# Loading two weights later and folding them inside the adjacency loop, in a graph layer followed by attention and experts

## The chip, the cores and the metric

The kernel runs on one core of one Trainium2 chip. The metric is the device time of one execution in microseconds (us), reported as the median of several runs. The core has five engines that run side by side, each through its own list of instructions in order: TensorE (PE in the profile; PEld is its weight load), VectorE (DVE), ScalarE (ACT), GpSimd (POOL) and SyncE (SP, which here only issues transfers). They wait for each other and for transfers on semaphores.

## The reference, cut to what matters

One layer takes x of 4096 nodes by 256 features and an adjacency matrix of 4096 by 4096. It has a graph part and then an attention part with a mixture of eight experts:

```
f   = layernorm(x)                                  # 4096 x 256
h   = adj @ (f @ neigh_W.T) / (adj.sum(axis=1) + 1)
x   = x + concat([f, h]) @ lin_W.T                  # = f @ L1 + h @ L2
x   = x + attention_and_experts(layernorm(x))
```

With lin_W.T split into its upper half L1 and its lower half L2, the second term is (adj @ f / deg) @ (neigh_W.T @ L2). The product of the two 256 x 256 weights does not depend on the data, so the kernel computes M = neigh_W.T @ L2 once. This product is what the change calls folding.

## The kernel before, in words

The graph part is written in manual order: each engine executes its instructions in the order in which the Python code emits them. The nodes are cut into NB = 8 blocks of 512 (four tiles of 128). An outer loop `aggregate(b, steps)` (L474) goes over the eight blocks of result nodes, and inside it the index jb goes over the eight blocks of neighbours. For each pair one block of adjacencies, 512 x 512 in float32 (1 MB), is loaded into one of three buffers (`load`, L258), and TensorE multiplies it with the normalised features of block jb. The product is arranged as seven products of 256 x 256 pieces in place of eight, which needs sums and differences of the pieces:

- `halve(n)` (L430) makes the sums and differences of adjacency block n on DVE (L441 to L444, 128 x 512 each). POOL adds the same sums up for the degrees (L449, L451).
- `halve_x(b)` (L403) does the same for the features of block b (L406 to L409).

Before a feature block can be used it has to be prepared. All of this happens during the first outer pass, b = 0:

- `load_x(b)` (L255) loads 512 rows of x.
- `scales_x(b)` (L385) takes the statistics: `stats` on DVE (L162, L164), then `power` on POOL (L168, L169), which gives 1/standard deviation.
- `normed_x(b, t)` (L391, instruction L393) normalises tile t on DVE.
- `turned_x(b)` (L398) transposes the normalised block on TensorE (L379), and ACT copies the result out of PSUM (L381).
- `features(b)` (L458) multiplies the transposed block with L1 on TensorE (L465, tiles pf, two halves). Between these matmuls it emits the four `normed_x` of block b + 1, and after each half DVE adds the result to x (L472).

In pass b = 0 the steps of preparation sit in the middle of each neighbour block, after the fourth of its seven products. At jb they are: `halve(jb + 1)`, `turned_x(jb + 2)`, `features(jb + 2)`, `halve_x(jb + 2)`, `scales_x(jb + 4)`. The step of jb = 3 also has `load_rest`, which issues seven small loads for the attention part. In the fourth block the features at hand are therefore those of block 5, and the neighbours whose `normed_x` stand in between are those of block 6.

`fold()` (L341) makes M in two halves: four matmul instructions L345 in the source (tiles pm; the trace shows eight passes, since a float32 matmul is recorded as two), and two copies L349 on ACT into m_sb. M is first used when the result of b = 0 is finished, during b = 1. The tiles pm and pf share one PSUM pool of two buffers, `p_pj`, with the tag "pj": a new tile takes the older of the two buffers, and its first matmul must wait until the last reader of the tile that was there is done. For a pf tile that reader is the DVE addition L472.

Before the loop the order is: first loads, then 26 transposes of the identity (L620, tile idle) which compute nothing that is used, then `fold()`, then blocks 0 and 1 of the features with the statistics of blocks 1, 2 and 3 and the sums of adjacency block 0. The weight neigh_W lies in qT[4] and L2 in qT[5], which are not used otherwise before the fifth result block is worked on or, for qT[5], before `turn_wo` in the step of jb = 6.

Transfers are issued by two engines: SP (x, adjacencies, neigh_W) and ACT (L2, L1). The instruction that issues may have to wait for a semaphore, and then everything behind it on that engine waits.

Of the kernel before, what the change touches and what calls it, by code (L numbers as in the profile page):

```python
# [17 lines left out]
P = 128  # L18
N = 4096
C = 256  # L20
# [46 lines left out]
def fast_kernel(  # L67
# [24 lines left out]
    nc = tc.nc  # L92
# [65 lines left out]
    def stats(pool, b, tiles=range(TB)):  # L158

        st = pool.tile([P, TB, nc.vector.BN_STATS_DIM], F32, tag="st", name=f"st_{b}_{tiles[0]}")  # L160
        for t in tiles:
            nc.vector.bn_stats(st[:, t, :], res[b][:, t, :])  # L162
        for t in tiles:
            nc.vector.bn_aggr(mv[b][:, t, :], st[:, t, :])  # L164

    def power(dst, src, scale, eps):

        nc.gpsimd.tensor_scalar(dst, src, scale, eps, op0=ALU.mult, op1=ALU.add)  # L168
        nc.gpsimd.tensor_tensor(dst, dst, half[:, 0 : dst.shape[1]], op=ALU.pow)  # L169
# [73 lines left out]
    with (  # L243
# [11 lines left out]
        def load_x(b):  # L255
            nc.sync.dma_start(res[b], x_blocks[b])

        def load(n):  # L258

            if n < NB * NB:  # L260
                blocks[n] = adjs.tile([P, TB, 512], F32, tag="a", name=f"a_{n // NB}_{n % NB}")
                nc.sync.dma_start(blocks[n], adj[n // NB, n % NB])
# [3 lines left out]
            nc.sync.dma_start(res[0][:, some], x_blocks[0][:, some])  # L266

        wn_sb, l2_sb = qT[4][:, :, 0:C], qT[5][:, :, 0:C]
        nc.sync.dma_start(wn_sb, neigh_w.rearrange("(c p) o -> p c o", p=P))
        nc.scalar.dma_start(l2_sb, lin_t[C : 2 * C, :].rearrange("(c p) o -> p c o", p=P))  # L270

        m_sb = gw.tile([P, 2, C], F32, name="m_sb")
        l1_sb = qT[6][:, :, 0:C]
# [1 line left out]
        for n in range(2):  # L275
            load_x(1 + n)
            load(n)
        for b in range(3, 6):
            load_x(b)
        tables = {}  # L280

# [59 lines left out]
        def fold():  # L341
            for c in range(2):
                pm = p_pj.tile([P, 512], F32, tag="pj", name=f"pm_{c}")
                for k in range(2):
                    nc.tensor.matmul(  # L345
                        pm[:, :C], wn_sb[:, k, c * P : (c + 1) * P], l2_sb[:, k, :],
                        start=(k == 0), stop=(k == 1),
                    )
                nc.scalar.copy(m_sb[:, c, :], pm[:, :C])  # L349
# [23 lines left out]
        def transposed(src, dst):  # L373

            for h in range(2):
                tr = p_tr.tile([P, 2, 2, P], F32, tag="tr", name="tr")
                for t in range(2):
                    for c in range(2):
                        nc.tensor.transpose(tr[:, c, t, :], src(2 * h + t, c), ident)  # L379
                cols = slice(h * 2 * P, (h + 1) * 2 * P)  # L380
                nc.scalar.copy(dst[:, :, cols], tr.rearrange("p c t i -> p c (t i)"))  # L381
# [3 lines left out]
        def scales_x(b, at_a_time=TB):  # L385
            for t in range(0, TB, at_a_time):
                some = slice(t, t + at_a_time)
                stats(gx, b, range(TB)[some])
                power(rstd[b][:, some], mv[b][:, some, 1:2], 1.0, EPS_LN)
# [8 lines left out]
        def turned_x(b):  # L398

            turned[b] = qT[b % 4]  # L400
            transposed(lambda t, c: g[b][:, t // 2 * 2 + c, t % 2, :], turned[b])

        def halve_x(b):  # L403

            part = [g[b][:, k] for k in range(7)]
            nc.vector.tensor_sub(part[T1], part[G12], part[G11])  # L406
            nc.vector.tensor_sub(part[T3], part[G22], part[G12])
            nc.vector.tensor_sub(part[T2], part[G22], part[T1])
            nc.vector.tensor_sub(part[T4], part[T2], part[G21])  # L409
# [20 lines left out]
        def halve(n):  # L430

            if n == NB * NB:
                return
            a = blocks.pop(n)
            m = {
                f"A{r + 1}{k + 1}": a[:, 2 * k : 2 * k + 2, r * 2 * P : (r + 1) * 2 * P]
                for r in range(2) for k in range(2)
            }
            m["S1"], m["S2"], m["S4"] = sums_at[n % 2]
            m["S3"] = m["A21"]  # L440
            nc.vector.tensor_add(m["S1"], m["A21"], m["A22"])  # L441
            nc.vector.tensor_sub(m["S2"], m["S1"], m["A11"])
            nc.vector.tensor_sub(m["S4"], m["A12"], m["S2"])  # L443
            nc.vector.tensor_sub(m["S3"], m["A11"], m["A21"])  # L444
            halves_of[n] = m
            jb = n % NB
            for i, k in ((0, 2), (1, 0)):
                if jb == 1:
                    nc.gpsimd.tensor_add(all_s[:, i], sums_at[(n - 1) % 2][k], sums_at[n % 2][k])  # L449
                elif jb > 1:  # L450
                    nc.gpsimd.tensor_add(all_s[:, i], all_s[:, i], sums_at[n % 2][k])  # L451
            if jb == NB - 1:

                ends = all_s[:, :, 0, :]
                nc.gpsimd.tensor_add(ends, ends, all_s[:, :, 1, :])
                nc.gpsimd.tensor_add(ends[:, 0], ends[:, 0], ends[:, 1])

        def features(b):  # L458
            fT = turned.pop(b)
            for h in range(2):  # L460
                pj = p_pj.tile([P, 2, C], F32, tag="pj", name=f"pf_{b}_{h}")
                for t in range(2):
                    for c in range(2):
                        at = (2 * h + t) * P
                        nc.tensor.matmul(  # L465
                            pj[:, t, :], fT[:, c, at : at + P], l1_sb[:, c, :],
                            start=(c == 0), stop=(c == 1),
                        )
                    if b + 1 < NB:
                        normed_x(b + 1, 2 * h + t)  # L470
                x1 = res[b][:, 2 * h : 2 * h + 2, :]
                nc.vector.tensor_add(x1, x1, pj)  # L472
# [145 lines left out]
        idle = p_pj.tile([P, TB, P], F32, tag="pj", name="idle")  # L618
        for n in range(26):
            nc.tensor.transpose(idle[:, n % TB], ident, ident)  # L620
        fold()
        load(2)
        for b in range(6, NB):
            load_x(b)
# [2 lines left out]
        features(0)  # L627
        halve_x(0)
        turned_x(1)
        scales_x(2)  # L630
        halve(0)
        features(1)
        halve_x(1)
        scales_x(3)
        steps = {jb: [] for jb in range(NB)}
        for jb in range(NB):
            for f, b in (
# [2 lines left out]
            ):  # L640
                if b < NB or f is halve:
                    steps[jb].append(lambda f=f, b=b: f(b))
        steps[3].append(load_rest)
        for jb, f in ((5, scale_rest), (6, turn_wo), (7, router_wo)):
            steps[jb].append(f)
        behind, at_end = [], []
        for b in range(NB):
            sums, degrees, linear = finish(b)
            if b:

                steps = {0: behind, (0, "end"): at_end}
# [1489 lines left out]
@with_exitstack  # L2141
def adj_ffn_kernel(ctx: ExitStack, tc: tile.TileContext, *args):
    nc = tc.nc
    kept = ctx.enter_context(tc.tile_pool(name="kept", bufs=1))
    left_over = kept.tile([1, 1], I32, name="left_over")
    table = kept.tile([P, 2, RARE], I32, name="rare_table")
    mine = kept.tile([P, RARE, NE], F32, name="rare_mine")
    lists = fast_kernel(tc, *args, left_over, table, mine)
    state = nc.values_load(left_over[0:1, 0:1], min_val=0, max_val=2)
    with tc.If(state != 0):  # L2150
        with tc.If(state == 2):
            general_kernel(tc, *args)
        with tc.If(state == 1):
            ln2, w13, w2, out = (args[i] for i in (8, 9, 10, 13))
            rare_groups(tc, ln2, w13, w2, out, lists, table, mine)
# [73 lines left out]
```

## Time and profile before

| | before |
|---|---|
| time, median of 3 runs | 1600.92 us (1599.28 to 1603.71) |
| profiled execution | 1608.9 us, span 1607.1 us |
| TensorE busy | 1584.9 us, 99% of the span |
| DVE busy | 1069.7 us, 67% |
| POOL busy | 617.4 us, 38% |
| ACT busy | 473.3 us, 29% |
| mean DMA rate over the span | 130 GB/s |

Busy time is the time in which an engine executes something, not the time in which it is at its peak. The shares are means over the whole span. For TensorE in the stretch from 30 to 60 us, where the features are prepared, the profile gives 29.17 us busy, and for DVE 29.38 us; from 200 to 300 us it is 100.00 and 70.60.

A row of the timeline gives the start and the length of a group of equal instructions that follow each other on an engine, the engine, the source line, the operation and its operands, how many there were, and, in brackets, how long the engine was idle before the group and what released it. "pf<-qT_all" means that tile pf is written from tile qT_all.

### The profile page before, as it was taken

The page shows a single profiled execution, that of the slowest core. Times are in us where ns is not written, and L with a number is a line of the kernel's source. Part 1 is how long each engine was busy: PE and PEld are TensorE (multiplying, and loading weights), DVE is VectorE, ACT ScalarE, POOL GpSimd, SP SyncE. Part 2 cuts the span into 40 slices and gives each one's busy share as a digit, 9 for nine tenths or more (in the row PEclk, how much of TensorE's full clock was granted, in tenths as well). Part 3 has the DMA queues.
Part 4 walks back from the last instruction along what each step waited for, and adds up shares of the span by engine and source line. Part 5 has one row for each costly group of instructions (what it writes and reads, how often), then busy time and mean ns, then how long its engine had stood idle before and what let it go on. Part 6 is the DMA issues. An engine that isn't in the chain of part 4 may idle for free. (4 is left out here: it accounts for less than half of the span.)

```text
span 1607.1 us, 22624 instructions
## 1 busy us (share of the span) xinstructions
PE 1584.9 (99%) x8404; PEld 1139.2 (71%) x8404; DVE 1069.7 (67%) x2055; ACT 473.3 (29%) x893; POOL 617.4 (38%) x726
## 2 busy tenths in 40 slices
PE   9999999999999999999999999999999999999997
PEld 8888888888888543344343434348889999989996
DVE  8966676676676688789889788884445453434443
ACT  1101001010010455554555545543112222222221
POOL 3445556556557341253433352412512222112113
PEclk9999999999999999999999999999999999999999
DMA  6333433434333000010100010176665776777784
GB/s 229 125 135 137 156 131 135 140 129 157 135 134 109 4 1 1 13 41 28 36 20 27 14 41 28 38 225 220 218 200 169 232 254 221 239 254 220 244 272 104
DMA packets 67991, 209.58 MB, mean 130 GB/s; under 512 B 14688, under 2 KB 46816, under 8 KB 54240
## 3 DMA queue, kind: packets, MB, share of 16 engines
q1 hardware_dynamic: 54608, 190.05, 34.1%
q0 software_dynamic: 12720, 17.47, 5.5%
q8 instruction: 68, 1.11, 0.3%
q10 hardware_dynamic: 544, 0.52, 0.1%
q14 instruction: 51, 0.42, 0.1%
HBM read 180.81 MB, written 31.42 MB: 132 GB/s over the span
## 5 line engine op out<-in xcount | busy, mean ns | idle before, releaser
L711 DVE TENSOR_TENSOR sum<-sum,pt 128x1024 f32<-128x1024 f32 (+3 forms) x258 | 298.1, 1155 | 17.7 <-ACT pt L693 0.5
L693 ACT ACTIVATE pt<-sc 128x1024 f32<-128x1024 f32 (+3 forms) x288 | 252.4, 958 | 177.5 <-PE sc L688 117.1
L688 PE MATMUL sc<-qT_all,kT 64*128 64x512 f32 (+3 forms) x1152 | 250.4, 569 | 1.4 <-ACT pt L693 0.4
L496 PE MATMUL acc<-a,g 128*128 128x256 f32 x1024 | 245.1, 380 | 0.0
L723 PE MATMUL ya<-pt,vv 128*64 128x512 f32 (+3 forms) x1152 | 242.6, 563 | 0.0
L1301 PE MATMUL h<-xT,qT_all 128*128 128x256 f32 (+1 forms) x1232 | 221.3, 339 | 0.7 <-DMA qT_all<-in_w_dram 0.7
L496 PEld LDWEIGHTS acc<-a,g 128*128 128x128 f32 x1024 | 193.4, 190 | 31.8 <-DVE vv L514 1.2
L1373 POOL DMA_INDIRECT acc_dram<-y,rows x57 | 89.8, 1575 | 317.1 <-DVE y L1368 85.1
L1301 PEld LDWEIGHTS h<-xT,qT_all 128*128 128x128 f32 x1232 | 196.5, 191 | 21.2 <-issue 2.3
L688 PEld LDWEIGHTS sc<-qT_all,kT 64*128 64x128 f32 x1152 | 103.8, 186 | 141.2 <-issue 107.5
L1308 DVE TENSOR_TENSOR hT<-si,h 128x256 f32<-128x256 f32 (+2 forms) x126 | 62.6, 507 | 185.8 <-ACT si L1307 184.2
L723 PEld LDWEIGHTS ya<-pt,vv 128*64 128x64 f32 x1152 | 76.2, 136 | 146.9 <-issue 139.8
L451 POOL TENSOR_TENSOR all_s<-all_s,more_sums 128x512 f32<-128x512 f32 x72 | 106.1, 1486 | 107.3 <-DVE more_sums L443 107.3
L1307 ACT ACTIVATE si<-h 128x256 f32<-128x256 f32 (+2 forms) x126 | 56.9, 453 | 281.6 <-PE h L1301 255.6
L496 PE MATMUL acc<-more_sums,g 128*128 128x256 f32 x512 | 126.2, 379 | 0.0
L907 POOL DMA_INDIRECT lists<-row,slots x64 | 70.7, 1105 | 115.8 <-issue 115.4
L1301 PE MATMUL h<-xT,res_all 128*128 128x256 f32 (+1 forms) x616 | 108.2, 334 | 0.0
L496 PEld LDWEIGHTS acc<-more_sums,g 128*128 128x128 f32 x512 | 97.2, 190 | 14.8
L1301 PEld LDWEIGHTS h<-xT,res_all 128*128 128x128 f32 x616 | 96.6, 191 | 9.0
L695 POOL TENSOR_SCALAR_AFFINE_SELECT pt<-pt 128x256 f32<-128x256 f32 x64 | 46.6, 754 | 116.0 <-ACT pt L693 115.2
L381 ACT COPY qT_all<-tr 128x512 f32<-128x512 f32 x30 | 16.1, 589 | 214.3 <-PE tr L379 214.3
L496 PE MATMUL acc<-qT_all,g 128*128 128x256 f32 x256 | 65.7, 379 | 0.0
(279 smaller groups left out, 2123.5 us busy)
## 6 DMA issues: line engine op xcount, KB each, us to landing
a<-in_adj_dram SPq DMA_DIRECT2D x64, 1024.0 KB
qT_all<-in_w_dram SPq DMA_DIRECT2D x28, 1408.0 KB
res_all<-in_w_dram SPq DMA_DIRECT2D x28, 768.0 KB
res_all<-in_w_dram SPq DMA_DIRECT2D x14, 1408.0 KB
qT_all<-in_w_dram SPq DMA_DIRECT2D x14, 768.0 KB
rows<-lists SPq DMA_DIRECT2D x25, 265.0 KB
lists<-pad SPq DMA_DIRECT2D x8, 662.5 KB
acc_dram<-res_all SPq DMA_DIRECT2D x8, 512.0 KB
```

The source lines that it names most:

```text
L451: nc.gpsimd.tensor_add(all_s[:, i], all_s[:, i], sums_at[n % 2][k])
L496: nc.tensor.matmul(acc[bank][:, at, :], g[jb][:, right, k, :], m[left][:, k, :], start=(jb == 0 and k == 0 and at == 0), stop=(jb == NB - ...
L688: nc.tensor.matmul(ps[:, j, :w], kT[sb][hd, i * P : (i + 1) * P], qT[b][hd, p, off:], start=True, stop=True,)
L693: nc.scalar.activation(pt[:, :, :w], ps[:, :, :w], AF.Exp, scale=HD ** -0.5)
L695: nc.gpsimd.affine_select(out=pt[:, :, 0:P], in_=pt[:, :, 0:P], pattern=[[0, 2], [1, P]], compare_op=ALU.is_ge, fill=0.0, base=0, channel_ ...
L711: nc.vector.tensor_add(sums[b, p][:, :, off:], before[:, :, off:], pt[:, :, : 512 - off])
L723: nc.tensor.matmul(accs[b, p][hd, off:], vv[sb][:, i, hd], pt[:, j, : 512 - off], start=(s == 0), stop=(s == TB * b + TB - 1),)
L907: put = nc.gpsimd.indirect_dma_start(out=lists[:, :], out_offset=bass.IndirectOffsetOnAxis(ap=chosen[b][:, k, t, :], axis=0), in_=flats[b] ...
L1301: nc.tensor.matmul(ps[:, m % 2, m // 2 - q, :], w13_sb[:, c, m * P : (m + 1) * P], xT[:, c, :], start=(c == 0), stop=(c == 1),)
L1307: nc.scalar.activation(si[:, 0:both, :], ps[:, 0, 0:both, :], AF.Silu)
L1308: nc.vector.tensor_mul(hT[:, q : q + both, :], si[:, 0:both, :], ps[:, 1, 0:both, :])
L1373: put = nc.gpsimd.indirect_dma_start(out=(acc_dram if k < NM - LAST else out)[:, :], out_offset=at, in_=y[:, h, :], in_offset=None, comput ...
```

## The change

It has four edits. The load of neigh_W moves from SP to ACT, and the loads of neigh_W and L2 are emitted after the loads of x blocks 1 to 3 and adjacency blocks 0 and 1; on ACT, the load of L1 now stands first. The call of `fold()` moves from the place ahead of block 0's transposes to the end of the step of jb = 3 (the fourth block of neighbours) in the first outer pass. `halve(0)` moves ahead of `scales_x(2)`, so DVE makes the first sums of adjacencies before the statistics of x block 2. The remaining line is only the x load of block 3, written apart.

```diff
-        nc.sync.dma_start(wn_sb, neigh_w.rearrange("(c p) o -> p c o", p=P))
-        nc.scalar.dma_start(l2_sb, lin_t[C : 2 * C, :].rearrange("(c p) o -> p c o", p=P))
...
         for n in range(2):
             load_x(1 + n)
             load(n)
-        for b in range(3, 6):
+        load_x(3)
+        nc.scalar.dma_start(wn_sb, neigh_w.rearrange("(c p) o -> p c o", p=P))
+        nc.scalar.dma_start(l2_sb, lin_t[C : 2 * C, :].rearrange("(c p) o -> p c o", p=P))
+        for b in range(4, 6):
             load_x(b)
...
-        fold()
         load(2)
...
         halve_x(0)
         turned_x(1)
+        halve(0)
         scales_x(2)
-        halve(0)
         features(1)
...
-        steps[3].append(load_rest)
+        steps[3].extend((load_rest, fold))
```

The lines of the file after the changed loads are numbered one higher: L379 becomes L380, L465 becomes L466, L472 becomes L473, and so on until the former place of `fold()`.

## The prediction

> **What bounds the kernel now.** I read the page first: TensorE is busy 99% of the span, in every slice, so time is won or lost only where TensorE stands still or gets more work.
>
> ```profile
> span 1607.1 us, 22624 instructions
> PE 1584.9 (99%) x8404; PEld 1139.2 (71%) x8404; DVE 1069.7 (67%) x2055; ACT 473.3 (29%) x893; POOL 617.4 (38%) x726
> PE   9999999999999999999999999999999999999997
> ```
>
> Then the waits of TensorE from 0 to 480 us, the whole graph part. They sum to 3.5 us, 1.4 of it before the first instruction; the rest is the 0.3 us ahead of each block's features. So behind the start there is no idle time that could take up a delay: a delay of TensorE there goes to the end.
>
> ```profile
> PE pf L465 <- ACT qT_all L381: 2.1, 8, 0.3
> PE idle L620 <- POOL ident masks.py:199: 1.4, 1, 1.4
> ```
>
> Third, the timeline of the first 60 us, where all four edits lie.
>
> ```profile
> 7.02 2.08 PE L345 MATMUL pm<-qT_all 128*128 128x256 f32 x8
> 8.88 1.41 DVE L162 BATCH_NORM_STATS2 st<-res_all 128x6 f32<-128x256 f32 x4 [0.45 <-DMA res_all<-in_x_dram]
> 11.98 0.73 DVE L393 TENSOR_SCALAR g<-res_all,mv,rstd 128x256 f32<-128x256 f32 x2 [1.41 <-POOL rstd L169]
> ...
> 16.16 1.40 DVE L162 BATCH_NORM_STATS2 st<-res_all 128x6 f32<-128x256 f32 x4
> 17.75 0.66 DVE L441 TENSOR_TENSOR qT_all<-a 128x512 f32<-128x512 f32 x1
> 18.55 1.46 POOL L169 TENSOR_TENSOR rstd<-rstd,half 128x4 f32<-128x4 f32 x1
> 20.38 0.73 DVE L393 TENSOR_SCALAR g<-res_all,mv,rstd 128x256 f32<-128x256 f32 x2
> 22.05 1.04 PE L379 MATMUL tr<-ident,g 128*128 128x128 f32 x8
> ```
>
> Between 8.43 and 11.98 DVE waits twice, for x block 1 (0.45 us) and for POOL's power (1.41 us). After 11.98 the timeline names no wait on DVE until 79.96 us: through all the preparation DVE works without a break, just ahead of TensorE in some products and behind it in others. Where it is behind is seen in the fourth block of neighbours (same view, from 55 to 82 us):
>
> ```profile
> 56.07 3.72 PE L465 MATMUL pf<-qT_all 128*128 128x256 f32 x16 [0.29 <-ACT qT_all L381]
> 59.41 0.84 PEld L496 LDWEIGHTS acc<-a,g 128*128 128x128 f32 x4
> 62.06 0.67 DVE L472 TENSOR_TENSOR res_all<-res_all,pf 128x512 f32<-128x512 f32 x1
> 63.31 0.67 DVE L472 TENSOR_TENSOR res_all<-res_all,pf 128x512 f32<-128x512 f32 x1
> 79.96 0.69 DVE L472 TENSOR_TENSOR res_all<-res_all,pf 128x512 f32<-128x512 f32 x1 [1.40 <-PE pf L465]
> ```
>
> TensorE has written both pf tiles of block 5 by 59.8, but DVE reads them only at 62.06 and 63.31. Today nobody waits for that, since the next tile of this two-buffer pool comes at 67.
>
> [...] 26 idle transposes take 5.81 us (0.22 each), the eight at 8.93 take 1.04 (0.13 each). [...] all 16 are busy from 2.5 us on, at 348 to 385 GB/s up to 5 us. [...] The trace has POOL's power at 1.01 us with DVE idle (10.94) and at 1.46 us beside DVE's sums (18.55).
>
> **The change part by part.**
>
> *Loads.* One SP issue (0.47 us) ahead of x block 1 goes; one more on ACT (0.5 us), whose first work comes at about 7.9. The ACT loads wait for no semaphore, so they still start within the first 2.5 us; "behind the adjacencies" holds in the text only. Ahead of the end of x block 1 stand the same bytes as before: x0 and x1 512 KB each and three weights of 256 KB, since the two issuers interleave. What changes is that x1 and L2 now run from two queues side by side. Before, neigh_W and x1 ran from one: 301 to 334 GB/s from 5.5 to 7 us, against about 380 with two. For 0.52 MB that is 1.69 against 1.38 us, so x1 may land 0.3 us sooner. Bounds: 0, and 0.45 (DVE isn't free before 8.43). I take 0.3, an estimate.
>
> *Fold removed at the start.* 2.08 us of TensorE go, and two ACT copies of 0.37. Transposes of block 0 need the first normalised tiles (7.10) and the last (8.43), so they end at about 8.75 instead of 9.97, and features(0) end near 12.4 instead of 13.9. But block 1's transposes need its normalised tiles, which hang on x1 and DVE: the last one is ready at 13.96, less 0.3. So features(1), from 15.04, start about 14.1: of 2.08 us about 1.0 is won, and the next part takes even that away.
>
> *halve(0) before the statistics of block 2.* Before, 4.22 us lie from the statistics (16.16) to normalising block 2 (20.38); POOL's power was hidden by the sums. Now: sums 2.63 (17.75 to 20.38), statistics 1.68 (16.16 to 17.84), then DVE waits for POOL with nothing to do, 1.40 as at 11.98 (10.58 to 11.98). Sum 5.71, so DVE is D = 1.49 us later from there on (bounds: 1.4, and 2.1 if the power ran at its 17.93 to 20.01 length). Queued behind the waiting DVE instruction are everything up to block 7, and TensorE's transposes for blocks 2 to 7. The gain is nothing: the first product that needs sums is reached at about 19.3 with 1.0 us won, and before the sums for it were ready at 19.14. TensorE's transposes of block 2 now end about 24.1 less 0.3, before 23.09: it stands 0.6 to 0.9 us behind the old schedule there. DVE does not catch that up before the fold, as its list had no gap.
>
> *Fold in the fourth block.* Eight passes at the steady 0.216 (four in 0.86: 59.63 to 60.49) are 1.73 us of work on a full engine. They also wait: pm 0 takes the buffer of pf 0 of block 5 and pm 1 that of pf 1, so pm 1 cannot start before the second L472 addition ends. The built order shows both waiting on DVE. In old times that is 63.31 + 0.67 = 63.98, + 0.05 to the weight load (as from ACT's copy to features), + 0.86 for pm 1 = 64.89, where the products before went on at 59.41: 5.48 us. Since the addition itself is late by D and early by x1's 0.3, the sum is 5.48 + 1.49 − 0.30 = 6.67 us. TensorE's own earlier or later arrival cancels, because DVE sets the moment. The two copies fall on an idle ACT and hide.
>
> Afterwards DVE has lead enough; it waits for features(6), and adjacency block 6, issued at 62.4 before and now some 6.8 later, lands near 78 while its sums are due only after features(6). Nothing gives time back: 1607.1 + 6.7 = 1613.8 for the profiled span. The profiled execution, span 1607.1, is 0.4% above the median of the three runs without a trace; a shift of a few us carries over to them unchanged (0.4% of 6.7 is nothing), so with the same sum rounded to 6.6 the forecast is 1600.92 + 6.6 = **1607.5 us**, slower by 0.41%.
>
> **The rivals.**
>
> *The fold costs its work alone.* The pool's buffers would be free in time; then 0.6 behind at block 2 + 1.73 = 2.3 to 2.7 us: 1603.4. For it: DVE would need to be 4.2 us earlier (63.98 against 59.8), and the timeline shows no such reserve. It decides where the second addition ends ahead of pf's last pass.
>
> *Not slower: the fold fits in TensorE's gaps.* If the loop with b = 0 were bound by DVE, which has 29.38 of 30 us there, the 1.73 us would lie beside it and the 1.0 won at the start would stay: 1599.9. It decides from about 2 us of TensorE waiting between 20 and 60 us. Against it: only 0.3 per block is seen, and that sits ahead of features, not at the fold.
>
> *A cold clock on top.* The stall at the fold is about 3.7 us (60.4 to 64.1 and a shorter one between halves)[...]. The same could happen to features(0) at the start, partly hidden behind DVE. 1609 to 1611.
>
> *The loads change nothing:* x1 lands as before, or a little later; the sum is then 6.97: 1607.9, inside the forecast.
>
> **How the numbers follow.** Forecast with its wait 0.70, clock on top 0.08, work alone 0.13, fits 0.06, anything else 0.03. Bounds of the forecast alone: 5.48 + 1.4 − 0.45 = 6.4 and 5.48 + 2.1 = 7.6; the three runs lie 4.4 us apart, so a median of such runs may be 1 to 1.5 off on either side. The range for 8 in 10 is 1603.0 to 1611.0, which takes in part of the work-alone case and of the cold clock. A measurement tells about 0.3%, 4.8 us, from no change. From the cases: slower 0.78 (both first, less what noise takes), same 0.18, faster 0.04.
>
> **What would show it.** Right: in the page, TensorE waits of some 4 us at the fold's line put down to DVE's addition L473; DVE waiting about 1.4 us for POOL's rstd ahead of normalising block 2; the first DVE statistics of block 1 at 8.5 to 8.9. Step by step: resumption of the fourth block's products near 66.1 instead of 59.4, and at every later point of the graph part the same lag. Wrong: additions of block 5 that end before TensorE gets there, a lag that shrinks after 80 us, or x1 landing over 1 us earlier.

## The result, and the profile after

The changed kernel takes 1612.42 us (median of 6 executions, 1607.15 to 1614.18) against 1602.04 for the kernel before. The ratio of the runs on record is 1.0058 with a 95% interval of 1.0033 to 1.0082 (it is not simply the quotient of the two medians, which is 1.0065): slower, by more than the forecast 1607.5 and outside its range of 1603.0 to 1611.0. Two later sets of the unaltered change gave 1607.24 against 1599.32 (ratio 1.0049, 1.0035 to 1.0063) and 1610.1 against 1601.09 (1.0051, 1.0033 to 1.0070). Both of these medians lie inside the forecast's range, so on which side of its limit a set falls is luck; what the forecast had wrong is seen in the traces of all three. The executions of one kernel spread over 6 to 12 us, so beside the times I use a landmark inside one trace: the start of the transposes tr_wo, the first unmoved TensorE work that comes a while after all four edits. It lies at 87.53 us before and at 97.63 after, 10.1 later.

The page of the changed kernel first: TensorE executes as many instructions as before (8404) and is busy 1.6 us longer (1586.5 against 1584.9), so the time was lost in standing still and in running slowly, not in more work.

```profile
PE 1586.5 (98%) x8404; PEld 1139.7 (71%) x8404; DVE 1069.6 (66%) x2055; ACT 473.9 (29%) x893; POOL 616.1 (38%) x726
```

The waits of TensorE from 0 to 480 us (who waited for whom: us in total, times, longest) name two that the kernel before did not have. The first is the fold's, for DVE's addition of the features; the second is the transposes', for the normalised features.

```profile
PE pm L346 <- DVE res_all L473: 3.7, 1, 3.7
PE tr L380 <- DVE g L394: 2.8, 4, 1.4
```

The timeline of the start (start, length, engine, line, operation; in brackets the idle time ahead and its releaser):

```profile
4.94 0.75 DVE L162 BATCH_NORM_STATS2 st<-res_all 128x6 f32<-128x256 f32 x2 [4.94 <-DMA res_all<-in_x_dram]
7.92 0.76 PE L380 MATMUL tr<-ident,g 128*128 128x128 f32 x4 [1.37 <-DVE g L394]
9.25 1.11 PE L380 MATMUL tr<-ident,g 128*128 128x128 f32 x4 [0.57 <-DVE g L394]
9.43 1.40 DVE L162 BATCH_NORM_STATS2 st<-res_all 128x6 f32<-128x256 f32 x4
10.15 4.80 PE L466 MATMUL pf<-qT_all 128*128 128x256 f32 x16
...
19.84 1.40 DVE L162 BATCH_NORM_STATS2 st<-res_all 128x6 f32<-128x256 f32 x4
22.93 0.73 DVE L394 TENSOR_SCALAR g<-res_all,mv,rstd 128x256 f32<-128x256 f32 x2 [1.41 <-POOL rstd L169]
```

The last row shows DVE's new wait for POOL's power, 1.41 us, where the forecast put it. The row at 9.43 has no bracket: DVE did not wait for x block 1 at all. What was late is block 0, at 4.94 against 4.11 before, and features(0) took 4.80 us where 16 passes took 3.72 before. The clock that was granted to TensorE had fallen to half speed, at 9.12 us, in the second of two pauses of only 1.37 and 0.57 us. A row of the view by stretches gives the stretch and its length, the busy time of PE, PEld, DVE, ACT and POOL with the number of instructions, and then the granted TensorE clock, the DMA share and GB/s:

```profile
10.00:12.50 2.50, 2.50 (x8) 2.05 (x7) 1.11 (x7) 0.59 (x1) 1.21 (x2) 0.50 1.10 394
```

At the fold (the timeline again, with the features of block 5 ahead):

```profile
57.88 3.72 PE L466 MATMUL pf<-qT_all 128*128 128x256 f32 x16 [0.29 <-ACT qT_all L382]
64.59 0.68 DVE L473 TENSOR_TENSOR res_all<-res_all,pf 128x512 f32<-128x512 f32 x1
65.32 3.78 PE L346 MATMUL pm<-qT_all 128*128 128x256 f32 x8 [3.73 <-DVE res_all L473]
65.84 0.68 DVE L473 TENSOR_TENSOR res_all<-res_all,pf 128x512 f32<-128x512 f32 x1
...
68.90 1.85 PE L497 MATMUL acc<-a,g 128*128 128x256 f32 x4
70.59 1.03 PE L497 MATMUL acc<-more_sums,g 128*128 128x256 f32 x4
```

TensorE idles for 3.73 us until the first addition has ended. Then the eight passes take 3.78 us, against 2.08 at the start of the kernel before, and the next four take 1.85 where the group after them takes 1.03: the array runs slowly after the pause. From start to start that is 0.45 and 0.42 us a pass (65.32 to 68.90, and 68.90 to 70.59), twice the steady 0.216. The granted clock fell while TensorE still stood, at 63.73, 2.1 us after its last work had ended at 61.60:

```profile
62.00:63.00 1.00, 0.00 (x0) 0.00 (x0) 1.00 (x2) 0.00 (x0) 1.00 (x1) 1.00 0.00 0
63.00:64.00 1.00, 0.00 (x0) 0.00 (x0) 1.00 (x2) 0.00 (x0) 1.00 (x2) 0.87 0.00 0
64.00:65.00 1.00, 0.00 (x0) 0.00 (x0) 1.00 (x2) 0.00 (x0) 0.52 (x1) 0.50 0.00 0
```

From there the lag stays: attention's scores start at 543.7 (before 533.6) and the first expert outputs of L1353 from res_all at 1132.0 (1121.8), both 10.1 to 10.2 later.

### The profile page after: what moved, and what is told of

Its sections match the earlier page's. It is cut to its first block, busy times and chain, and to the rows that moved or that the text cites. A ratio compares the mean times of both kernels' runs of the same rounds, so it can differ in the third digit from the quotient of the medians.

```text
span 1612.1 us, 22622 instructions
## 1 busy us (share of the span) xinstructions
PE 1586.5 (98%) x8404; PEld 1139.7 (71%) x8404; DVE 1069.6 (66%) x2055; ACT 473.9 (29%) x893; POOL 616.1 (38%) x726
```

## The experiments

My theory after the result: the wait for the pf buffers is the largest term, the late DVE chain the next, and the slow clock after the pause makes up what the forecast missed. Rivals: the loads made the start late; or the moved work is dear by itself. The landmark and the times, each time against the kernel before, run beside it:

| kernel | tr_wo starts | median, us | ratio (95%) |
|---|---|---|---|
| before | 87.53 | 1602.04, 1599.32 to 1601.09 beside the runs below | |
| the change, three sets | 97.63, 96.42, 96.68 | 1612.42, 1607.24, 1610.1 | 1.0058, 1.0049, 1.0051 |
| e1 fold late only | 94.27 | 1606.25 | 1.0044 (1.0030 to 1.0058) |
| e2 change, fold in other pool | 89.95 | 1601.42 | 1.0017 (1.0009 to 1.0024) |
| e3 change, pause filled | 94.12 | 1605.95 | 1.0054 (1.0036 to 1.0072) |
| e4 order of DVE only | 88.33 | 1599.92 | 1.0005 (0.9994 to 1.0015) |
| e6 loads only | 88.82 | 1604.39 | 1.0032 (1.0013 to 1.0051) |
| e7 fold late, other pool, rest old | 88.48 | 1600.25 | 1.0009 (1.0000 to 1.0018) |
| e8 x first, fold in a gap | 87.17 | 1601.15 | 1.0006 (0.9995 to 1.0017) |
| e10 pure delay | 94.91 | 1609.15 | 1.0051 (1.0033 to 1.0070) |

**e1: the fold alone.**

```diff
-        fold()
-        steps[3].append(load_rest)
+        steps[3].extend((load_rest, fold))
```

> The kernel before, with only the fold moved to the fourth block; loads and the order of DVE as before. Read at the start of tr_wo (before 87.53 us, after 97.63). Theory (the wait for the pf buffers is the main term, the rest comes from the DVE chain and a cold clock): VectorE stays on its old schedule to within 0.5 us, so the second addition of block 5 ends near 64.0 and TensorE waits about 2.9 us[...]; tr_wo starts at 93.0 (+5.5), 95.1 if the clock goes cold all the same; time +5 to +6 us over before. Rival (the fold costs its eight passes and the large delay comes from the loads and the order): tr_wo at 89.3, time +2.

Measured: tr_wo at 94.27, +6.9 us in the median. The addition ended at 63.87, as expected, and the rival's 89.3 is out. But the clock fell here too: it averages 0.98 over the first 100 us, against 1.00 in e7, and the fold's passes take 3.32 us against 1.89 there. The timeline of this kernel:

```profile
62.67 3.32 PE L345 MATMUL pm<-qT_all 128*128 128x256 f32 x8 [3.57 <-DVE res_all L472]
65.78 1.61 PE L496 MATMUL acc<-a,g 128*128 128x256 f32 x4
```

The pause is 3.57 us rather than 2.9, because TensorE came to the fold earlier (it had no fold at the start), while DVE kept its schedule. Coming earlier won nothing; it only lengthened the pause.

**e2: the fold without a wait for DVE.** All of the change, but the fold's tiles come from the pool whose readers are done.

```diff
-                pm = p_pj.tile([P, 512], F32, tag="pj", name=f"pm_{c}")
+                pm = p_tr.tile([P, 512], F32, tag="tr", name=f"pm_{c}")
```

> The changed kernel, but the fold's two tiles take buffers of the other pool (tag tr), whose readers, the copies on ScalarE, are long done. Theory: no wait for VectorE at the fold and so no cold clock; left are the lag at block 2 (1.9 us in the changed kernel's trace, 25.24 against 23.33) and eight warm passes (1.7): tr_wo at 91.2, time +3.6 over before, 6.5 below the changed kernel. Rival (the delay is the work and the late DVE chain, whatever the pool): tr_wo stays at 97, time +10.

Measured: 89.95, 6.5 us below the second trace of the change and 1.25 below my own figure. The timeline at the fold:

```profile
56.76 3.72 PE L466 MATMUL pf<-qT_all 128*128 128x256 f32 x16 [0.29 <-ACT qT_all L382]
60.32 1.89 PE L346 MATMUL pm<-qT_all 128*128 128x256 f32 x8
62.05 1.03 PE L497 MATMUL acc<-a,g 128*128 128x256 f32 x4
```

No bracket ahead of pm: the eight passes start when features(5) are done, take 1.73 to the next start, and the next four are at full speed. DVE's additions still come at 63.52 and 64.76, and nobody waits for them. So 6.5 us of the delay hang on the buffers; the passes themselves and the late DVE chain make up the 2.4 that are left.

**e3: the pause filled.** The change with 16 unused transposes ahead of the fold.

```diff
+            for n in range(16):
+                nc.tensor.transpose(filler[:, n // 2 % 2, n % 2], ident, ident)
...
+        steps[3].extend((load_rest, fill, fold))
```

> The changed kernel with 16 transposes of the identity, unused, ahead of the fold (2.1 us of work at 0.13 each) inside the wait for the buffers. Theory (the clock fell during the 3.7 us of idleness and cost 2.1): the idle stretch is at most 1.7 us, the eight passes of the fold take 2.1 instead of 3.8 and the next four 1.0 instead of 1.9; tr_wo at 95.5, time 2 us below the changed kernel. Rival (the slow passes have another cause, or the clock has nothing to do with it): 97.6 or later, up to 99.7 if the transposes add to the path.

Measured: tr_wo at 94.12. First the timeline of this kernel, then the stretch from 50 to 75 us, of this kernel and of the change's second run:

```profile
60.08 1.91 PE L646 MATMUL filler<-ident 128*128 128x128 f32 x16
64.01 2.37 PE L346 MATMUL pm<-qT_all 128*128 128x256 f32 x8 [2.02 <-DVE res_all L473]
66.22 1.03 PE L497 MATMUL acc<-a,g 128*128 128x256 f32 x4
```

```profile
50.00:75.00 25.00, 22.28 (x116) 18.95 (x115) 23.23 (x47) 2.89 (x6) 12.79 (x11) 1.00 0.36 116
```

```profile
50.00:75.00 25.00, 20.95 (x90) 17.54 (x89) 23.14 (x47) 1.82 (x4) 12.27 (x11) 0.86 0.35 110
```

Both kernels wait for the same two additions; the second one, which pm 1 needs, started at 64.52 and 64.45. With an idle stretch of 2.02 us the granted clock stayed at 1.00; with 3.76 it averaged 0.86 over these 25 us. The difference at the landmark is 96.42 − 94.12 = 2.3 us: the price of the slow clock. More work in the wait brought the landmark forward. The whole times can't tell it: the ratio is 1.0054 against 1.0049 for the change, with intervals that overlap. The lowest executions point the same way: e3's is 6.8 us above before's, those of the three sets of the change 8.1 to 8.3.

**e4: the order of DVE alone.**

```diff
+        halve(0)
         scales_x(2)
-        halve(0)
```

> The kernel before, with only halve(0) ahead of scales_x(2). Theory: VectorE waits 1.4 us for POOL before normalising block 2 and is 1.5 us later from there; TensorE reaches block 2's transposes at 22.05 as before and waits there, so tr_wo starts about 1.2 later, 88.7; time +1.2, not to be told from before. Rival (no effect: the wait on POOL is made up): 87.5. Rival (it is the main cause): 90 or more.

Measured: 88.33, +0.8. DVE waits 1.41 us for POOL ahead of block 2, and TensorE waits for it in two pieces, 0.25 and 0.57:

```profile
21.92 0.73 DVE L393 TENSOR_SCALAR g<-res_all,mv,rstd 128x256 f32<-128x256 f32 x2 [1.41 <-POOL rstd L169]
22.48 0.67 PE L379 MATMUL tr<-ident,g 128*128 128x128 f32 x4 [0.25 <-DVE g L393]
...
23.72 0.67 PE L379 MATMUL tr<-ident,g 128*128 128x128 f32 x4 [0.57 <-DVE g L393]
```

So alone the edit costs 0.8 us. Without the fold at the start TensorE comes to block 2 earlier and waits longer: in e2 the two pieces are 1.00 and 0.57 us. At the fold of the change, DVE sets the moment, and the edit counts with its full 1.4.

**e5: the change again.**

> The changed kernel unaltered, run again beside the others. Read at the start of tr_wo (before 87.53, changed kernel 97.63). Theory (the first profile caught a late x block 0, at 4.94 against 4.42 to 4.62 in the runs since, and a cold clock in features(0), 4.80 us against 3.62): with x0 at about 4.5 and features(0) warm the second addition of block 5 ends at 65.2 as in the run with filled wait, and tr_wo starts at 96.2, since only the cold clock of the fold comes on top of that run's 94.1; time +7 to +10. Rival (the change itself makes x0 late): first statistics at 4.9 or later again, tr_wo at 97.6.

Measured: first statistics at 4.35, features(0) in 3.62, tr_wo at 96.42. The late block 0 of the first profile and the slow clock in features(0) did not come back. At the fold it is the same picture as in the first trace:

```profile
63.94 3.78 PE L346 MATMUL pm<-qT_all 128*128 128x256 f32 x8 [3.76 <-DVE res_all L473]
67.52 1.91 PE L497 MATMUL acc<-a,g 128*128 128x256 f32 x4
```

**e6: the loads alone.** Edit: the first two hunks of the change's diff.

> The kernel before with only the order of the loads changed as in the change (fold at the start, halve(0) behind the statistics). Theory (the bytes ahead of x block 1 are the same): first statistics between 4.1 and 4.6 as in the runs with the old loads, those of block 1 at about 8.6 with at most 0.3 us of waiting, the fold not later than before; tr_wo at 87.2 to 88.0, time the same within 0.1%. Rival (the loads are what makes the changed kernel's start late): first statistics at 4.9, tr_wo 1 us later; the fold waiting for L2.

Measured: first statistics at 4.43, those of block 1 at 8.63 without a wait, but tr_wo at 88.82, outside my 87.2 to 88.0. Part of the rival holds: with the fold still at the start, TensorE waits for L2, which is now the third load of its issuer.

```profile
PE pm L346 <- DMA qT_all<-in_lin_t_dram: 1.3, 1, 1.3
```

In the full change this wait is gone, since the fold comes 55 us later. The median of 1604.39 is not what the landmark says (+1.3): the lowest of its nine executions is 1599.93, against 1598.76 for before, and that is the one with a trace. Six of the nine lie 4 to 12 us above it, with a mean granted clock of 0.995 to 0.998 against 0.999; where they lost this was not traced.

**e7: the fold late, free of the wait, all else old** (the edits of e1 and e2 on the kernel before).

> The kernel before, with only the fold in the fourth block and its tiles in the other pool, so it waits for nobody: no changed loads, old order of DVE. Theory: the fold costs its eight warm passes, 1.73, less the 0.5 to 0.8 that TensorE is earlier at block 1's features; tr_wo at 88.6 (range 88.3 to 89.3), time +1. Against the run with the fold alone, 94.3, this shows the whole price of the pool's wait and its cold clock: 5.7. Rival (moving the fold costs more than its passes by itself, for instance at the start): 90 or more.

Measured: 88.48, as expected; the median is 0.9 us above before, with an interval from 1.0000 to 1.0018. Between this and e1, 94.27, only the pool differs: 5.8 us.

**e8: a try at a faster start.** On the kernel before; also `fold()` in the other pool, behind `features(0)`, and 20 idle transposes for 26.

```diff
-        nc.sync.dma_start(wn_sb, neigh_w.rearrange("(c p) o -> p c o", p=P))
-        nc.scalar.dma_start(l2_sb, lin_t[C : 2 * C, :].rearrange("(c p) o -> p c o", p=P))
...
+        load_x(1)
+        nc.sync.dma_start(l1_sb, lin_t[0:C, :].rearrange("(c p) o -> p c o", p=P))
+        nc.sync.dma_start(wn_sb, neigh_w.rearrange("(c p) o -> p c o", p=P))
+        nc.sync.dma_start(l2_sb, lin_t[C : 2 * C, :].rearrange("(c p) o -> p c o", p=P))
+        load(0)
```

> An attempt at a faster start on the kernel before: all early loads on SP in the order x0, x1, L1, neigh_W, L2, adjacency 0; 20 unused transposes in place of 26; the fold right behind features(0), in the other pool, where TensorE waits for block 1. Theory (the start hangs on x0, x1 and the VectorE chain): x0 lands about 1 us sooner, statistics of block 1 near 7.6, and features(1) start at about 14.5 against 15.04; tr_wo at 87.0, time -0.5, below what can be told. Rival (L1 and the weights behind x1 come too late and TensorE waits for them): tr_wo at 88 or more.

Measured: first statistics at 3.60, those of block 1 at 7.41, features(1) at 14.68, tr_wo at 87.17: 0.4 us sooner than before. In time it can't be told from before (1.0006, 0.9995 to 1.0017). The statistics of block 1 began 1.5 us earlier than before, but then the fold stood in TensorE's way: the last normalised tile of block 1 was ready at 12.48, and its transposes began at 13.41, when the fold's passes were through. I did not find a version that beats both kernels.

**e9: the change a third time.**

> The changed kernel unaltered, a third time, for the spread of its time: the first six executions had a median of 1612.42, the next five 1607.24, and the trace of each has the same lag to within 1.3 us at tr_wo (97.63, 96.42). Theory (the difference is a wait for transfers in the expert stage that comes in some executions of every kernel): most executions at 1607 +- 1, some 4 to 7 above, median within 1606.5 to 1609, +7 to +9 over before; tr_wo at 96 to 98. Rival (the change's true cost is +10 and the second set was lucky): median at 1611 or more.

Measured: tr_wo at 96.68; six executions from 1606.84 to 1615.69, median 1610.1, +9.0 over before. That is above my 1609 and below the rival's 1611, so neither of my two figures was hit; the landmark and the lowest execution (+8.3 over before's lowest, 1598.55) agree with the theory.

**e10: a pure delay.** The kernel before with 68 unused transposes at the fold's new place.

> The kernel before with nothing changed but 68 unused transposes on TensorE at the place of the fold (68 times 0.128 = 8.7 us), so a lag of 8.7 without waits, clock or loads. Theory (a lag made at 60 us goes to the end whole, and nothing downstream takes it up or adds to it): tr_wo at 96.2, median +8 to +9 over before, the same spread above the lowest as before's. Rival (later stages give some of it back): under +6; rival (a later start of the expert stage makes its waits more frequent): lowest at +8.7, median at +11 or more.

```profile
59.58 7.59 PE L646 MATMUL filler<-ident 128*128 128x128 f32 x68
67.00 1.03 PE L496 MATMUL acc<-a,g 128*128 128x256 f32 x4
```

The transposes took 7.4 us to the next start, not 8.7 (0.109 each). The 0.13 of the expectation was the length of a row of eight over its count, in which the end of the last one weighs; between rows of 4, 8 and 16 (0.60, 1.04 and 1.91 us) each further transpose adds 0.11 too. tr_wo is 7.4 later, the lowest execution is 8.2 above before's and the median 8.1. A lag at 60 us goes to the end whole; these times show nothing downstream that takes it up. The spread of its six executions is 5.8 us, before's 6.5: no sign that a lag widens it.

## Why the prediction was wrong, point by point

**The sign and the largest term held.** Slower was right, and so was the fold's wait for the pf buffers. Taking the second trace of the change, the second addition ends at 64.45 + 0.68 = 65.13; the forecast's 63.98 + 1.49 − 0.30 is 65.17. The run with a warm clock at the fold, e3, is 6.59 late at the landmark, the forecast's sum 6.67. Part of this closeness is luck: the 0.30 had the right size for a wrong reason, as told below.

**The step that failed is the last term behind that addition: 0.86 us for pm 1 at the steady 0.216 a pass.** The clock fell in the pause, so pm and the products behind it ran at half speed. The forecast named this as a rival, "A cold clock on top", and gave it 0.08. The low share was the author's estimate; no trace of before showed it. The pause came out as forecast (3.73, 3.76 and 3.73 in the three traces of the change), and the clock fell in all three (a mean of 0.86 from 50 to 75 us in each), and in e1 with 3.57 (0.98 over the first 100 us). It did not in e3 with 2.02 (1.00 from 50 to 75 us). The size was 2.3 us at the landmark (e3 against e5). With it the sum is 6.67 + 2.3 = 9.0, against 8.9 and 9.15 measured at tr_wo in the second and third traces.

**The stretch ahead of a fall was not idle.** The records of the granted clock in the first profile of the change and in that of before have three falls to 0.50 ahead of the end of the program: at 9.12 us (features(0)) and at 63.73 (the fold) in the change, and at 1437.57 in before. The clock stayed at half for 3.41, 6.83 and 3.41 us. In the 3.41 us ahead of each of them TensorE was busy for 1.60, 1.28 and 1.12 us. The length of a pause alone did not decide. The kernel before has two longer pauses behind 1400 us (waits of TensorE):

```profile
PE tx L1210 <- DVE vv L1286: 3.0, 1, 3.0
PE ye_y L1272 <- DVE y L1368: 2.3, 1, 2.3
```

The one of 2.3 us, from 1434.33, was followed by the fall at 1437.57. The one of 3.0, from 1569.63, was not: in the 3.41 us that ended with it TensorE had worked 0.45, and the clock stayed at 1.00 up to 1601 us. So the work left in the stretch does not decide by itself either; what parts these cases was not shown. In e3 the filler put 1.91 us of work into the time in which TensorE would otherwise have stood, and there the clock stayed at 1.00.

**The size.** The rival's 1609 to 1611 lie 1.5 to 3.5 us above the forecast; this was the author's estimate, and no trace of before showed it for the fold. In the first trace of the change the clock was at half for 6.83 us, of which TensorE worked 5.24. Half of that is 2.6. Less the 0.5 that the fold's passes lost at the full clock too in e3 (2.37 us against 1.89 in e2), since pm 1 stood for the second addition, this gives 2.1 as an estimate, near the 2.3 measured. In e1 less was lost: its clock averages 0.98 over the first 100 us, that of the second trace of the change 0.97.

**D, the wait for POOL, was right.** 1.41 us in every kernel with the new order, against 1.40.

**x block 1 sooner by 0.3 was not measured as such.** In the second trace its statistics start at 8.60 against 8.88, straight behind the normalisation of block 0, without a wait. But e4 and e1, with the old loads, show 8.64 and 8.86 and no wait either: DVE waited where block 0 landed at 4.11 (before) and not where it landed at 4.34 or later, and that time varied between 4.11 and 4.94 over the eleven traces other than e8's, 4.11 to 4.62 with the old loads and 4.35 to 4.94 with the new. Only e8, which puts x alone in front, moved it (3.60). So the loads gave nothing that these traces can tell at the start, and the 0.45 us wait in the profile of before, on which the term rested, was that execution's. The 0.3 was not a gain of the change.

**"The fold costs its work alone"** is what e2 shows when the wait is taken away: +2.4 at the landmark (forecast of that rival 2.3 to 2.7). It was the right price for the wrong kernel.

**The sum at the landmark**, each term the difference of two traces, one of each kernel: late fold without a wait 88.48 − 87.53 = 0.95 (e7); loads and order 89.95 − 88.48 = 1.5 (e2 over e7); the wait for the buffers with a warm clock 94.12 − 89.95 = 4.2 (e3 over e2, with the fill inside the wait, and the other pool in e2); the slow clock 96.42 − 94.12 = 2.3 (e5 over e3). Together 8.9.

**Small slips of the forecast.** The sum of 6.67 was rounded to 6.6; 6.7 would give 1607.6. And 0.13 us for a transpose is a row's length over its count; from start to start it is 0.11.

**The rest of 1612.42.** Of the 4.9 us between it and 1607.5, 1.1 lie in the kernel before, whose median was 1602.04 and not 1600.92, and 2.3 in the clock at the fold; what is left is within the spread of six executions. The landmark of the first trace holds 1.2 us more than the second, from the late block 0 and the slow clock in features(0), which e5 and e9 don't show. The forecast had named this too ("The same could happen to features(0)"). The +7.9 and +9.0 of the later sets lie within the first set's interval of 5.3 to 13.1 us (0.33 to 0.82% of 1602). Whether the clock fell at the fold in all seventeen executions of the change was not traced; three were. Where single executions lose 4 to 7 us more is seen in the traces behind 1400 us, the experts: e9's TensorE waits 2.9 us for DVE at L1368 and the granted clock is 0.98 from 1400 to 1500; before's own profile has the 3.0 and 2.3 us shown above and 0.98 there, e4's no wait of TensorE behind 1400. What sets it off was not tried and stays open; e10 gives no sign that a lag by itself does.

## What to carry to other kernels

Before moving a step, look whose buffer its output takes: here a computation of 1.7 us cost 6.7 at the landmark when it was moved alone (e1), because its tile had to wait for the last reader of another tile, on an engine that ran late; a pool with free buffers left 1.0 of that (e7). Work that partly fills a gap at the start costs less there, 0.8 of its 1.7 us here, and its full price on an engine that is full. And when the forecast itself contains a pause of TensorE, weigh the slow clock as a term of the sum: here it followed each of the four pauses of 3.57 to 3.76 us at the fold and cost about 2.3 us in the change, and the falls of the first profiles came with 1.12 to 1.60 us of TensorE work in the 3.41 us ahead.

## What the runs showed of the hardware

- With the pauses of 3.57 to 3.76 us at the fold the granted clock fell in four of four traces: its mean from 50 to 75 us was 0.86 in each of the three of the change, and in e1 it was 0.98 over the first 100 us. In the first trace it was 0.50 from 63.73 to 70.56 us; TensorE worked 5.24 us of that, with 0.42 to 0.45 us a pass against 0.216. In the change this cost about 2.3 us at the landmark (e5 against e3).
- The three falls in the first profiles of the change and of before came behind 3.41 us with 1.60, 1.28 and 1.12 us of TensorE work, and half speed lasted 3.41, 6.83 and 3.41 us.
- Pauses of 2.0 (e3) and 3.0 us (before) were not followed by a fall, one of 2.3 us (before) was.
- With 16 unused transposes (1.91 us) ahead of the fold the granted clock from 50 to 75 us was 1.00 (e3), without them 0.86 (e5). In e10, 68 of them followed each other every 0.109 us at 1.00.
- In before two DMA queues ran side by side while loads of SP and ACT were on their way: from 3 to 4 us they moved 189 and 214 packets, at 380 GB/s together. From 5.5 to 7 us one ran alone, at 314. The mean busy share of the 16 DMA engines was 0.99 to 1.09 from 2.5 to 5 us.
